# Layer 1 of four chained attention layers in narrower TensorE tiles, with its keys and values computed once per half, and another order of the first loads and of some pieces

## The chip, the cores and the metric

The kernel runs on one core of one Trainium2 chip. A core has TensorE (matrix products into PSUM), VectorE, ScalarE, GpSimd and SyncE, each with its own instruction stream, and DMA engines that move data between device memory and the on-chip memories. The metric is the device time of one execution in microseconds. The kernel before took 3054.2 us, the median of three runs (3051.49 to 3056.47).

## The reference

The input x has 4 images of 64 x 64 pixels and 64 channels, all float32. Four attention layers follow each other; the output of one is the input of the next.

```python
# layer 0: full attention, 4096 x 4096 scores per image; softmax over the last axis, then summed over the queries
q, k, v = x @ Wq + bq, x @ Wk + bk, x @ Wv + bv           # each (4096, 64)
attn = softmax(einsum('bic,bjc->bij', q, k), axis=-1)
x = gamma * einsum('bmn,bmc->bnc', attn, v) + x

# layer 1: 4096 queries of 8 channels, 1024 pooled keys and values (8 and 32 channels)
theta = x @ sn(w_theta)                                    # (4096, 8)
phi = maxpool2x2(x @ sn(w_phi))                            # (1024, 8)
g = maxpool2x2(x @ sn(w_g))                                # (1024, 32)
attn = softmax(theta @ phi.T, axis=-1)
x = x + sigma * ((attn @ g) @ sn(w_o) + b_o)

# layers 2 and 3: group norm, then full attention with 4096 x 4096 scores, projection, residual
```

`sn` divides a weight by its spectral norm estimate. The sums of exponentials are kept, and a count of partitions in which one is out of range selects a second, slower path; it does not run here.

## The kernel before, in words

An image lies on chip as 128 partitions x 2048: partitions 0 to 63 hold the 64 channels of one half of the pixels, 64 to 127 the channels of the other half. `half(i)` is a half of the partitions, `quarter(q)` 32 of them, `chunk(c)` 512 columns, `wide(j)` 1024 columns. NC is 4 (chunks), NB 32 (blocks of 128 keys).

The program is written in the order in which each engine runs it (`manual_schedule`), so the order of the Python statements is the order of each engine's queue. Foreground work is an attention of one layer for one image: `layer0`, `layer2` and `layer3` each run 64 calls of `step` (line 784). One step issues two groups of scores (`first`, lines 916 and 1115: four 64x64 products of 512 columns, then an exponential on ScalarE), and the products with the values for two earlier groups (`adds` and `then`). All other work is background: Python generators that yield MID or END, and `advance` (line 777) resumes the generator in the middle of a step, between the two groups of value products, or at its end. `background(tempo, ...)` sets which generators run under an attention; `drain` runs what is left when the attention is over. `before` and `due` are dictionaries from step number to work. Layer 1 is background: image 0's under layer 0 of image 1, with `bank=False`, because layer 0 keeps all four accumulator banks; the others' under layer 2 of the image before, with `bank=True`, an accumulator of their own.

PSUM has two buffers named s (`s_tile`, 128 x 1024 each), shared by all scores, projections and transposes, and four accumulators (`acc_tile`).

What the change touches, in the order of the file:

- `load_x` (643) loads an image in 16 DMAs (8 parts x 2 halves of the pixel blocks, for image 0). `load_form` (684) loads Wq and Wk, yields, then loads bq. For image 0 the loads of x alternate between SyncE's queue (SP) and ScalarE's; `load[0]` is ScalarE's queue until line 1394.
- `quadratic_form` (708) makes the product of Wq and Wk, and the bias column, once. `transposed` (861) turns x, `project` (826) makes queries, `first_queries` (879) the first half of image 0's queries in two arrangements, q and q_swapped.
- `layer1` (982): `project` gives theta in four copies at partitions 0, 32, 64 and 96. The loop at line 994 projects keys and values, one chunk at a time: the weight `wpg1` holds, for each of four quarters, phi in 8 columns and a quarter of g in 8 columns, so each quarter has all keys; `tensor_reduce` (1002) pools into `pg`. Eight transposes (1009) turn pg, and line 1010 copies g out of them with keys on partitions.
- `scores(j, k)` (1017): for a block of 128 keys, four products of 8 rows x 128 columns x 512, one per quarter, into two s buffers; two exponentials; from k = 1 on VectorE adds the exponentials into `zacc1` (1031). `add(j, k)` (1033) multiplies by g: into an accumulator, or, without a bank, into an s buffer, which VectorE then adds to `os[j]` (1049). `normalise` (1053) sums zacc by a product with ones (1056), takes reciprocals, and multiplies (1067); `last` (1070) applies w_o by two 128x128 products of 512 columns (1073) and adds to x1.
- The loop from line 1086 issues `scores` of unit n and `add` of unit n-1, 16 units an image and one more.
- `attention` (1106) is layer 2's and 3's loop. `turn` (1168) turns the result, copies the sums to the check columns and scales; `last` in `layer3` (1377) adds the residual and stores. At the end (1591 to 1616) the checks over all columns but the last eight run when the last attention has been issued; `rest_in_range` (1601) covers the last eight and writes the flag `bad`, called from `turn` by `after_sums`.
- At 1445 to 1456 the weights `wth1`, `wpg1` and two `wo1` are cleared and filled.

Of the kernel before, what the change touches and what calls it, by code (L numbers as in the profile page):

```python
# [11 lines left out]
ALU = mybir.AluOpType  # L12
AX = mybir.AxisListType
# [584 lines left out]
def fast_path(tc: tile.TileContext, a: dict, out: bass.AP, bad):  # L598
# [13 lines left out]
    P = 128  # L612
# [29 lines left out]

    def load_x(st, parts=((slice(None), lambda i: nc.sync.dma_start),)):
        st["xin"] = t = x_tile("xin").rearrange("p (k i c) -> p k i c", i=2, c=C)
        src = tokens(x[st["b"]])
        for ks, queue in parts:
            for r in range(4):
                for i in range(2):
                    queue(i)(t[r * W2 : (r + 1) * W2, ks, i, :], src[r, :, ks, i, :])

# [33 lines left out]
    def load_form(n, at, wq, wk, bq):  # L684
        w, b = scratch[:, at : at + P].rearrange("p (j f) -> p j f", j=2), scratch[0:C, at + P : at + P + 1]
        load[0](w[0:C, 0, :], wq)
        load[0](w[0:C, 1, :], wk)
        yield
        load[0](b, bq.rearrange("(c o) -> c o", o=1))
        form[n] = w, b, scratch[0:C, at + P + 1 : at + 3 * P + 1].rearrange("p (j f) -> p j f", j=2)  # L690

    form0 = load_form(0, 0, a["L0_conv_Wq"], a["L0_conv_Wk"], a["L0_conv_bq"])
    next(form0)
    load_x(state[0], [(ks, lambda i: (nc.sync, nc.scalar)[i].dma_start) for ks in (slice(0, 8), slice(8, 16))])
    ident = ctile([P, P], "ident")
# [28 lines left out]
    blocks = {n: (ctile([P, P], f"A{n}"), ctile([P, 1], f"Ab{n}")) for n in (0, 3)}  # L724
    for _ in form0:
        pass
    wv0 = diagonal("wv0", a["L0_conv_Wv"])
# [254 lines left out]
    def layer1(on, st, bank):  # L982
# [9 lines left out]
        rest = x_tile("pg")  # L992
        pg, g = rest[:, 0:M], rest[:, M : M + NK * 32].rearrange("p (k f) -> p k f", f=32)
        for c in range(NC):
            yield MID
            s = s_tile()
            for i in range(2):
                for d in range(2):
                    nc.tensor.matmul(  # L999
                        s[half(d), chunk(i)], wpg1[half(i), half(d)], x1[half(i), chunk(c)], start=True, stop=True  # L1000
                    )
            nc.vector.tensor_reduce(
                pg[:, ds(c * 256, 256)].rearrange("p (a b) -> p a b", b=16),
                s.rearrange("p (a i b j) -> p a b i j", i=2, b=16, j=2), AX.XY, ALU.max,
            )
        yield MID
        s = s_tile()
        for k in range(NK):
            nc.tensor.transpose(s[:, ds(k * P, P)], pg[:, ds(k * P, P)], ident)
        nc.vector.tensor_copy(  # L1010
            g.rearrange("p k (q f) -> p k q f", q=4),
            s.rearrange("p (k q f) -> p k q f", q=4, f=32)[:, :, :, D8 : 2 * D8],
        )

        ps, accs, zaccs, os = {}, {}, {}, {}

        def scores(j, k):
            ss = [s_tile() for e in range(2)]
            for e in range(2):
                for i in range(2):  # L1020
                    r = slice((2 * e + i) * 32, (2 * e + i) * 32 + D8)
                    nc.tensor.matmul(ss[e][:, chunk(i)], pg[r, ds(k * P, P)], th[r, chunk(2 * j + i)], start=True, stop=True)  # L1022
            ps[j, k] = pk = [p_tile() for e in range(2)]
            for e in range(2):
                nc.scalar.activation(pk[e], ss[e], AF.Exp)  # L1025
            if k == 1:
                zaccs[j] = x_tile("zacc1").rearrange("p (e f) -> p e f", e=2)
            if k >= 1:
                for e in range(2):
                    z = zaccs[j][:, e, :]  # L1030
                    nc.vector.tensor_tensor(z, ps[j, 0][e] if k == 1 else z, pk[e], ALU.add)  # L1031

# [37 lines left out]
        def last(j):  # L1070
            s = s_tile()
            for e in range(2):
                nc.tensor.matmul(s[:, chunk(e)], wo1[e], os[j], start=True, stop=True)  # L1073
            del os[j]
# [11 lines left out]
        for n in range(len(todo) + 1):  # L1086
            yield END if bank else MID
            if n < len(todo):
                scores(*todo[n])
            if n:  # L1090
                if not bank:
                    yield END
                add(*todo[n - 1])
            if n == NK:
                end = finish(0)
# [10 lines left out]
    def attention(st, turned_by, arranged, last, not_before, name):  # L1106
# [61 lines left out]
        def turn(c):  # L1168
# [14 lines left out]
            nc.vector.reciprocal(r_columns, z_columns)  # L1183
            if c == NC - 1 and "after_sums" in st:
                st["after_sums"]()
            t = os[c] = o_p.tile([P, 2 * 4, C], FP, tag="turned", name="turned")
# [184 lines left out]
    def layer3(st, not_before):  # L1371
# [5 lines left out]
        def last(c, t):  # L1377
            ks, i = slice(c // 2 * 8, c // 2 * 8 + 8), c % 2
            nc.vector.tensor_tensor(t, t, hb[:, ks, i, :], ALU.add)
            for r in range(4):  # L1380
                queue = nc.scalar if c == NC - 1 and st["b"] == B - 1 and r % 2 else nc.sync
                queue.dma_start(dst[r, :, ks, i, :], t[r * W2 : (r + 1) * W2, :, :])

        return attention(st, wv3, "p (i n) f -> p n i f", last, not_before, "done3")
# [6 lines left out]
    s0, s1, s2, s3 = state  # L1391
    alone(transposed("both", s0), quadratic_form(0, 1.0))
    alone(first_queries(s0))
    load[0] = nc.sync.dma_start

# [27 lines left out]

    for _ in load_form(3, 4 * P, a["L3_conv_wq"], a["L3_conv_wk"], a["L3_conv_bq"]):
        pass
    wv3, bv3 = ctile([P, P], "wv3"), ctile([P, C], "bv3")
# [19 lines left out]

    wth1, wpg1 = ctile([P, P], "wth1"), ctile([P, P], "wpg1")
    wo1 = [ctile([P, P], f"wo1_{e}") for e in range(2)]
    for t in (wth1, wpg1, *wo1):
        nc.gpsimd.memset(t, 0.0)  # L1450
    spectra = (
        ("theta", [(wth1[:, q * 32 : q * 32 + D8], every, slice(0, D8)) for q in range(4)]),
        ("phi", [(wpg1[:, q * 32 : q * 32 + D8], every, slice(0, D8)) for q in range(4)]),
        ("g", [(wpg1[:, q * 32 + D8 : q * 32 + 2 * D8], every, slice(q * D8, q * D8 + D8)) for q in range(4)]),
        ("o", [(wo1[q // 2][quarter(q), half(q % 2)], quarter(q), slice(0, C)) for q in range(4)]),
    )
# [133 lines left out]
    drain()  # L1590
    layer3(s3, free)

    last_column = checks[0]
    in_range, least = ctile([P, 2 * 4 + 2], "in_range"), ctile([P, 1], "least")
    for i, (seen, bound) in enumerate(((all_z, SUM_MAX), (all_r, 1.0 / SUM_MIN))):
        nc.vector.tensor_scalar(seen[:, 0:last_column], seen[:, 0:last_column], bound, None, ALU.is_le)
        nc.vector.tensor_reduce(in_range[:, 8 + i : 9 + i], seen[:, 0:last_column], AX.X, ALU.min)

    def rest_in_range():
        count = 2 * 4
        assert checks[0] == NCHECK and last_column == NCHECK - count
        nc.vector.tensor_scalar(in_range[:, 0:count], all_z[:, -count:], SUM_MAX, None, ALU.is_le)
# [7 lines left out]

    s3["after_sums"] = rest_in_range
    while due or urgent:
# [52 lines left out]
```

## Time and profile before

| what | value |
|---|---|
| median of three runs | 3054.2 us |
| profiled execution | 3055.06 us |
| its span, first to last instruction | 3053.3 us |
| mean granted TensorE clock | 0.997 |
| TensorE products busy | 3007.8 us, 99% |
| VectorE busy | 1775.9 us, 58% |
| ScalarE busy | 1945.8 us, 64% |
| mean DMA rate | 8 GB/s |

The page gives busy time of each engine, the span in 40 slices, the DMA queues, the chain of work that ended last, the costliest groups of instructions and the DMA issues. PE is TensorE's products, PEld its weight loads, DVE VectorE, ACT ScalarE, POOL GpSimd, SP SyncE; a q behind the name is the engine's queue. In a row of the timeline stand the start, the time taken, the engine, the line, the operation, what is written and read, shapes and a count, and in brackets the idle time before it and what ended that. A product row's bar contains a tail that overlaps the next product, so lengths of bars do not add up; starts do.

### The profile page before, as it was taken

How to read it: one execution, taken by the hardware profiler on the slowest of the kernel's cores; microseconds unless marked ns; L12 is line 12 of the kernel's file. 1: busy time of each engine (PE TensorE's matmuls, PEld its weight loads, DVE VectorE, ACT ScalarE, POOL GpSimd, SP SyncE). 2: the span in 40 equal slices, each digit the busy share in tenths (PEclk: the TensorE clock that was granted, in tenths of full speed). 3: DMA queues.
4: the chain of work that ended last, by engine and by line, in shares of the span. 5: the costliest groups of instructions: out<-in, count | busy, mean ns of one | idle time of the engine just before them, and what ended most of it. 6: DMA issues, size and time to landing. Idle time of an engine off the chain costs nothing.

```text
span 3053.3 us, 62809 instructions
## 1 busy us (share of the span) xinstructions
PE 3007.8 (99%) x27549; PEld 1133.9 (37%) x27549; DVE 1775.9 (58%) x2066; ACT 1945.8 (64%) x2815; POOL 37.0 (1%) x36
## 2 busy tenths in 40 slices
PE   8999999999999999999999999999999999999998
PEld 3333223423444442344443233333343334333333
DVE  1221332578731068772107787777887777877776
ACT  6877767665577856557885655555555555555554
POOL 0000000000000000000000000000000000000000
PEclk9999999999999999999999999999999999999999
DMA  2010000000001000000000000000000000000000
GB/s 36 1 29 1 1 1 1 15 1 1 15 1 29 1 1 1 11 5 2 15 1 1 1 1 15 19 5 5 8 19 5 19 2 1 7 17 5 8 5 9
DMA packets 41433, 24.62 MB, mean 8 GB/s; under 512 B 39744, under 2 KB 39744, under 8 KB 39744
## 3 DMA queue, kind: packets, MB, share of 16 engines
q1 hardware_dynamic: 37744, 19.77, 3.2%
q8 instruction: 218, 3.57, 0.5%
q10 hardware_dynamic: 3408, 0.76, 0.1%
q14 instruction: 63, 0.52, 0.1%
HBM read 4.79 MB, written 4.19 MB: 3 GB/s over the span
## 4 chain that ended last, share of the span: by engine, by line
PE 92%; DVE 4%; ACT 2%; issue 1%; DMA 0%; ACTq 0%; SPq 0%; DVEq 0%
PE s L1120 28%; PE acc L1154 28%; PE acc L948 14%; PE s L923 14%; PE s L1022 2%; DVE zacc L1131 2%; ACT p L1025 2%; DVE zacc L1031 1%; PE s L835 1%; PE s L1177 1%; PE s L854 1%; PE s L1073 1%; PE s L1265 0%; PE s L999 0%; ACT p L1125 0%
## 5 line engine op out<-in xcount | busy, mean ns | idle before, releaser
L1125 ACT ACTIVATE p<-s 128x1024 f32<-128x1024 f32 x1024 | 994.7, 1022 | 707.7 <-PE s L1120 699.1
L1131 DVE TENSOR_TENSOR zacc<-zacc,p 128x1024 f32<-128x1024 f32 x960 | 1173.5, 1222 | 377.3 <-ACT p L1125 339.6
L927 ACT ACTIVATE p<-s 128x1024 f32<-128x1024 f32 x512 | 519.6, 1015 | 53.1 <-PE s L923 34.1
L1154 PE MATMUL acc<-p,v 64*64 64x512 f32 x4096 | 519.0, 591 | 0.0
L948 PE MATMUL acc<-p,vs 64*64 64x512 f32 x4096 | 514.7, 591 | 1.0 <-ACT vs L937 1.0
L1120 PE MATMUL s<-q,k 64*64 64x512 f32 x2048 | 501.4, 598 | 8.9 <-ACT p L1025 5.4
L923 PE MATMUL s<-xT,q_swapped 64*64 64x512 f32 x2048 | 491.2, 592 | 6.2 <-DVE o L1049 5.7
L1154 PE MATMUL acc<-p,hT 64*64 64x512 f32 x4096 | 494.4, 590 | 0.0
L923 PE MATMUL s<-xT,q 64*64 64x512 f32 x2048 | 490.7, 592 | 2.2 <-DVE v L855 0.6
L1120 PE MATMUL s<-q,xT 64*64 64x512 f32 x2048 | 487.2, 589 | 0.0
L1120 PE MATMUL s<-q,k_swapped 64*64 64x512 f32 x2048 | 481.8, 598 | 0.7 <-DVE turned L1187 0.7
L1120 PE MATMUL s<-q,h_swapped 64*64 64x512 f32 x2048 | 479.3, 589 | 0.0
L929 DVE TENSOR_REDUCE all_z<-z 128x1 f32<-128x4 f32 x128 | 20.1, 157 | 625.1 <-ACT p L927 625.1
L937 ACT ACTIVATE vs<-v,all_r 64x64 f32<-64x64 f32 x512 | 176.6, 345 | 150.8 <-PE acc L948 73.7
L948 PEld LDWEIGHTS acc<-p,vs 64*64 64x64 f32 x4096 | 170.4, 133 | 257.1 <-issue 191.4
L1154 PEld LDWEIGHTS acc<-p,v 64*64 64x64 f32 x4096 | 172.0, 133 | 249.8 <-issue 241.3
L1154 PEld LDWEIGHTS acc<-p,hT 64*64 64x64 f32 x4096 | 157.8, 133 | 262.7 <-issue 261.9
L923 PEld LDWEIGHTS s<-xT,q_swapped 64*64 64x64 f32 x2048 | 146.7, 133 | 157.9 <-issue 111.8
L1120 PEld LDWEIGHTS s<-q,h_swapped 64*64 64x64 f32 x2048 | 144.5, 133 | 140.7 <-issue 135.0
L1120 PEld LDWEIGHTS s<-q,xT 64*64 64x64 f32 x2048 | 144.0, 133 | 139.5 <-issue 137.5
L923 PEld LDWEIGHTS s<-xT,q 64*64 64x64 f32 x2048 | 146.5, 133 | 132.3 <-issue 107.9
L1120 PEld LDWEIGHTS s<-q,k 64*64 64x64 f32 x2048 | 137.1, 133 | 157.6 <-issue 98.9
(204 smaller groups left out, 1615.3 us busy)
## 6 DMA issues: line engine op xcount, KB each, us to landing
k_swapped<-k SPq DMA_DIRECT2D x8, 512.0 KB, 5.4
h_swapped<-xT SPq DMA_DIRECT2D x8, 512.0 KB, 5.3
out_dram<-turned SPq DMA_DIRECT2D x62, 64.0 KB, 1.8
xin<-in_x_dram SPq DMA_DIRECT2D x24, 128.0 KB, 4.1
q_swapped<-q SPq DMA_DIRECT2D x6, 512.0 KB, 5.4
xin<-in_x_dram SPq DMA_DIRECT2D x8, 64.0 KB, 2.4
xin<-in_x_dram ACTq DMA_DIRECT2D x8, 64.0 KB, 2.6
out_dram<-turned ACTq DMA_DIRECT2D x2, 64.0 KB, 3.2
```

The lines of the kernel that those rows point to most:

```text
L835: nc.tensor.matmul(s[half(e), chunk(i)], w[half(i), half(e)], rhs[half(i), chunk(2 * j + (1 - e if exchanged else e))], start=True, stop=True,
L854: nc.tensor.matmul(s[:, ds(k * P, P)], rhs[:, ds((g * 8 + k) * P, P)], w, start=True, stop=True)
L923: nc.tensor.matmul(s[half(e), chunk(i)], queries(m, i, e), k[half(i), chunk(c)], start=True, stop=True)
L927: nc.scalar.activation(p, s, AF.Exp, accum_out=zs[m][:, c : c + 1])
L937: nc.scalar.activation(vs[half(e), :], v[half(e), m, :], AF.Copy, scale=rz[half(e), m : m + 1])
L948: nc.tensor.matmul(acc[c][half(i), :], vs[half(e), :], ps[2 * t + n][half(e), chunk(i)], start=(m == 0 and e == 0), stop=(m == NB - 1 and ...
L1022: nc.tensor.matmul(ss[e][:, chunk(i)], pg[r, ds(k * P, P)], th[r, chunk(2 * j + i)], start=True, stop=True)
L1025: nc.scalar.activation(pk[e], ss[e], AF.Exp)
L1120: nc.tensor.matmul(s[half(e), chunk(i)], k[(j + i) % 2][half(i), ds(j // 2 * P + e * C, C)], q[half(i), chunk(c)], start=True, stop=True,)
L1125: nc.scalar.activation(p, s, AF.Exp)
L1131: add = lambda: nc.vector.tensor_tensor(zaccs[c], p0, p, ALU.add)
L1154: nc.tensor.matmul(accs[c][e][half(i), :], v[half(e), j, :], p[half(e), chunk(i)], start=(j == 0), stop=(j == NB - 1),)
```

## The change

- The first loads: bq comes with Wq and Wk, all three on ScalarE's queue ahead of x; of x's first half only two of eight DMAs go to ScalarE's queue, the rest and the whole second half to SP's, and all later loads of weights to SP's.
- The first pieces: the quadratic form is issued ahead of the transposes; then transposes of the first half of x, its queries, the transposes of the second half, and the other arrangement of the queries.
- Layer 1's keys and values: `wpg1` is 64 columns wide, phi twice and g once in the gaps. One group of products takes two chunks, so there are two groups and two poolings per image instead of four, and `pgs[0]` holds one half of the keys in the upper 64 partitions, the other half in the lower. Two DMAs write the same with the halves exchanged into `pgs[1]`. Four transposes instead of eight, two copies instead of one, and one more yield.
- Layer 1's scores: eight products of 8 rows x 64 columns instead of four of 128 columns; the column half is the outer loop. The additions into zacc are returned as a function and called behind `add`.
- Layer 1's last products: w_o as one 128x128 tile of four 64x64 blocks, four products instead of two.
- `after_sums` becomes `after`, called when the last output's DMAs have been issued; the checks over the earlier columns run six steps before the end of the last attention.

```diff
-    form0 = load_form(0, 0, a["L0_conv_Wq"], a["L0_conv_Wk"], a["L0_conv_bq"])
-    next(form0)
-    load_x(state[0], [(ks, lambda i: (nc.sync, nc.scalar)[i].dma_start) for ks in (slice(0, 8), slice(8, 16))])
+    load_form(0, 0, a["L0_conv_Wq"], a["L0_conv_Wk"], a["L0_conv_bq"])
+    load[0] = nc.sync.dma_start
+    on_scalar = lambda r, i: nc.scalar.dma_start if i and r >= 2 else nc.sync.dma_start
+    load_x(state[0], [(slice(0, 8), on_scalar), (slice(8, 16), lambda r, i: nc.sync.dma_start)])
...
-        pg, g = rest[:, 0:M], rest[:, M : M + NK * 32].rearrange("p (k f) -> p k f", f=32)
-        for c in range(NC):
+        pgs = rest[:, 0 : M // 2], rest[:, M // 2 : M]
+        g = rest[:, M : M + NK * 32].rearrange("p (k f) -> p k f", f=32)
+        for j in range(NC // 2):
             yield MID
             s = s_tile()
             for i in range(2):
                 for d in range(2):
                     nc.tensor.matmul(
-                        s[half(d), chunk(i)], wpg1[half(i), half(d)], x1[half(i), chunk(c)], start=True, stop=True
+                        s[half(d), chunk(i)], wpg1[half(i), :], x1[half(i), chunk(2 * j + d)], start=True, stop=True
                     )
             nc.vector.tensor_reduce(
-                pg[:, ds(c * 256, 256)].rearrange("p (a b) -> p a b", b=16),
+                pgs[0][:, ds(j * 256, 256)].rearrange("p (a b) -> p a b", b=16),
                 s.rearrange("p (a i b j) -> p a b i j", i=2, b=16, j=2), AX.XY, ALU.max,
             )
+        for d in range(2):
+            nc.sync.dma_start(pgs[1][half(d), :], pgs[0][half(1 - d), :])
         yield MID
         s = s_tile()
-        for k in range(NK):
-            nc.tensor.transpose(s[:, ds(k * P, P)], pg[:, ds(k * P, P)], ident)
-        nc.vector.tensor_copy(
-            g.rearrange("p k (q f) -> p k q f", q=4),
-            s.rearrange("p (k q f) -> p k q f", q=4, f=32)[:, :, :, D8 : 2 * D8],
-        )
+        for n in range(NK // 2):
+            nc.tensor.transpose(s[:, ds(n * P, P)], pgs[0][:, ds(n * P, P)], ident)
+        by_key = s[:, 0:512].rearrange("p (k f) -> p k f", f=C)
+        nc.vector.tensor_copy(g[:, :, 0:24], by_key[:, :, 8:32])
+        nc.vector.tensor_copy(g[:, :, 24:32], by_key[:, :, 40:48])
+        yield MID
...
         def scores(j, k):
             ss = [s_tile() for e in range(2)]
-            for e in range(2):
-                for i in range(2):
-                    r = slice((2 * e + i) * 32, (2 * e + i) * 32 + D8)
-                    nc.tensor.matmul(ss[e][:, chunk(i)], pg[r, ds(k * P, P)], th[r, chunk(2 * j + i)], start=True, stop=True)
+            n, d = divmod(k, 2)
+            for m in range(2):
+                for e in range(2):
+                    for i in range(2):
+                        r = slice((2 * e + i) * 32, (2 * e + i) * 32 + D8)
+                        nc.tensor.matmul(
+                            ss[e][half(m), chunk(i)], pgs[0 if e == d else 1][r, ds(n * P + m * C, C)],
+                            th[r, chunk(2 * j + i)], start=True, stop=True,
+                        )
...
-            if k >= 1:
-                for e in range(2):
-                    z = zaccs[j][:, e, :]
-                    nc.vector.tensor_tensor(z, ps[j, 0][e] if k == 1 else z, pk[e], ALU.add)
+            zs = [ps[j, 0][e] if k == 1 else zaccs[j][:, e, :] for e in range(2)]
+            def accumulate():
+                for e in range(2):
+                    nc.vector.tensor_tensor(zaccs[j][:, e, :], zs[e], pk[e], ALU.add)
+            return accumulate
...
         def last(j):
             s = s_tile()
             for e in range(2):
-                nc.tensor.matmul(s[:, chunk(e)], wo1[e], os[j], start=True, stop=True)
+                for i in range(2):
+                    nc.tensor.matmul(s[half(i), chunk(e)], wo1[half(e), half(i)], os[j][half(e), :], start=True, stop=True)
...
-            if n < len(todo):
-                scores(*todo[n])
+            accumulate = scores(*todo[n]) if n < len(todo) else None
             if n:
                 if not bank:
                     yield END
                 add(*todo[n - 1])
+            if accumulate:
+                accumulate()
...
-    alone(transposed("both", s0), quadratic_form(0, 1.0))
-    alone(first_queries(s0))
-    load[0] = nc.sync.dma_start
+    st0 = transposed("both", s0)
+    next(st0)
+    alone(quadratic_form(0, 1.0))
+    next(st0)
+    queries0 = first_queries(s0)
+    next(queries0)
+    next(queries0)
+    alone(st0)
+    alone(queries0)
...
-    s3["after_sums"] = rest_in_range
+    s3["after"] = rest_in_range
+    before.setdefault(now[0] + NC * NB // 2 - 6, []).append(most_in_range)
+    layer3(s3, free)
```

## The prediction

> **What bounds the kernel now.** I read the page's busy times first, then its chain.
>
> ```profile
> PE 3007.8 (99%) x27549; PEld 1133.9 (37%) x27549; DVE 1775.9 (58%) x2066; ACT 1945.8 (64%) x2815; POOL 37.0 (1%) x36
> ...
> PE 92%; DVE 4%; ACT 2%; issue 1%; DMA 0%; ACTq 0%; SPq 0%; DVEq 0%
> ```
>
> TensorE is busy for 99% of the span and carries 92% of the chain, so TensorE time added or removed is span, and work of other engines counts only where TensorE waits for it. The groups of instructions by shape, TensorE only (shapes, count, busy us, mean ns), show what the change touches:
>
> ```profile
> L1022 PE MATMUL s<-th,pg 8*128 8x512 f32 x512 | 83.4, 639 | 0.2 <-ACT p L927 0.2
> L1040 PE MATMUL acc<-p,pg 128*32 128x512 f32 x384 | 51.1, 605 | 0.0
> ...
> L999 PE MATMUL s<-xT,wpg 64*64 64x512 f32 x128 | 19.1, 589 | 0.0
> ...
> L1073 PE MATMUL s<-o,wo 128*128 128x512 f32 x32 | 15.9, 618 | 0.0
> ...
> L1009 PE MATMUL s<-ident,pg 128*128 128x128 f32 x32 | 4.4, 280 | 0.0
> ```
>
> An fp32 product of 512 columns is two records. Records of one tile follow each other at 0.43 us while their own bars, with tails, are 0.59; so I measure slots, from the start of one group to the start of the next. Four 64x64 tiles run at once: 16 records (two score groups) take 1.72 us, one group of four products 0.86. Those are the pure prices below. Next, the timeline of one layer-1 unit inside an attention (images 1 to 3):
>
> ```profile
> 619.50 1.90 PE L1154 MATMUL acc<-p,v 64*64 64x512 f32 x16
> ...
> 621.33 1.14 PE L1022 MATMUL s<-th,pg 8*128 8x512 f32 x8
> ...
> 622.40 1.06 PE L1040 MATMUL acc<-p,pg 128*32 128x512 f32 x8
> 622.50 1.94 ACT L1025 ACTIVATE p<-s 128x1024 f32<-128x1024 f32 x2 [1.73 <-DVE zacc L1131]
> ...
> 623.58 0.14 PEld L1120 LDWEIGHTS s<-q,k 64*64 64x64 f32 x2 [1.02 <-ACT p L1025]
> 623.58 0.65 PE L1120 MATMUL s<-q,k 64*64 64x512 f32 x2
> ```
>
> A step runs from 617.68 to 623.58, 5.90 us, against 5.16 of pure products (1.72+1.72+0.86+0.86). The other 0.74: 0.11 ahead of L1022 (619.50 to 621.33 is 1.83, not 1.72), 0.21 between L1022 and L1040 (1.07), 0.32 behind L1040 (1.18), 0.10 within the scores. The pair behind L1040 waits for the exponential (ACT p L1025), which itself starts at 622.50, when L1022's bars end (621.33+1.14). So the end of the layer-1 scores, not only TensorE's slots, sets the step.
>
> **The change part by part.** The sum starts from the profiled execution, 3055.06 us (span 3053.3 and 1.8 around it), 0.9 above the median of 3054.2.
>
> 1. Projections of keys and values. The four groups at L999 per image become two. A slot is 0.86 (602.93 to 603.78), no wait in it: 4 images x 2 x 0.86 = 6.9. Eight pooling reductions of 1.22 on VectorE go too, off the path.
>
> 2. Eight transposes at L1009 become four. Eight take a slot of 1.02 (607.49 to 608.51), 0.16 of it the switch of tile shape: 4 x 0.43 = 1.7. Two copies replace one of 0.43 on VectorE; the added yield moves the first scores a step on, so nothing waits for them. Building the narrower weights drops one clear on GpSimd and four small products on VectorE, both idle there under layer 0: 0.
>
> 3. The swap of halves by two DMAs on SP. Nearest row: k_swapped, 512 KB, 5.4 us from issue to landing. Issued when the last reduction ends (605.4 in this stage), needed by the first scores, which the yield puts two steps later, near 613: 7.5 us of cover, and both DMAs are half that size. Cost 0. If the cover went, a TensorE wait of up to 5 us per image, 20 in all. Behind them on SP lie only the next q_swapped and k_swapped, needed a stage later.
>
> 4. Scores in 32x64 tiles: eight products where there were four, half as wide, so the same array time if all eight run together. The loads shrink from 182 ns (128 columns) to 133 (64), and the first product of a group waits for its load: L1022's first bars are 692 ns against 587 for its second, L1120's 640 against 589, so 0.105 falls to 0.05. Neighbouring tiles start 7 ns apart; four more give back 0.03 at the end. In a 5.90 step the exponential starts some 0.03 to 0.05 earlier: 48 units x 0.04 = 2. Bounds: +3 (stagger alone) and, if the array needs no switch between 64x64 and 32x64, another 64 x 0.11 = -7. No row shows two shapes with equal columns side by side, so I take the 0.11 as staying, as it does at every other switch.
>
> [...]
>
> 5. Image 0 (no PSUM bank; sums go through VectorE). Timeline of a steady step:
>
> ```profile
> 339.13 2.36 DVE L1031 TENSOR_TENSOR zacc<-zacc,p 128x1024 f32<-128x1024 f32 x2 [4.16 <-ACT p L1025]
> ...
> 340.42 0.65 PE L923 MATMUL s<-xT,q_swapped 64*64 64x512 f32 x2
> ...
> 341.41 0.68 DVE L1049 TENSOR_TENSOR o<-o,s 128x512 f32<-128x512 f32 x1
> ...
> 342.14 0.65 PE L923 MATMUL s<-xT,q_swapped 64*64 64x512 f32 x2 [0.64 <-DVE o L1049]
> ```
>
> The step is 7.12 us (333.30 to 340.42). The second score pair waits for L1049, queued behind L1031's two additions (2.36): its slot is 2.64 where unhindered ones are 1.77. With the additions behind it, L1049 runs at 340.55 to 341.23 and the 0.85 wait goes. What is late next is ScalarE: the second exponential still ends 3.3 us into the step and layer-1's second score buffer with it; with the column half outermost, the first buffer's products now also wait for that (1.1 us later than before), and L1040 for their exponential, 0.18. My step is 6.72; the trace's own steps without the VectorE wait are 6.72 too (319.92 to 326.64). Eight steps are 7.12: 8 x 0.40 = 3.2. Against it, at 411 L1067 moves behind two additions, 2.3 us, and ScalarE's L1068, and behind that the vs scalings that L948 needs, wait for it: 1.5. Net 1.7; bounds +2 and -7 (all 8 waits of 0.85).
>
> 6. Last products. Timeline, TensorE, around one:
>
> ```profile
> 713.10 1.04 PE L1154 MATMUL acc<-p,v 64*64 64x512 f32 x8
> 714.07 1.98 PE L1073 MATMUL s<-o,wo 128*128 128x512 f32 x4
> 715.98 1.09 PE L1154 MATMUL acc<-p,v 64*64 64x512 f32 x8
> ```
>
> The switch in (0.97-0.86), four 128x128 records in sequence (1.91) and the switch out (0.91-0.86) become one 64x64 group of 0.86: 0.11+1.05+0.05 = 1.2, 8 times, 9.7.
>
> 7. First loads and pieces.
>
> ```profile
> 6.82 1.94 PE L868 MATMUL s<-ident,xin 128*128 128x128 f32 x8 [6.82 <-DMA xin<-in_x_dram]
> ...
> 14.42 3.69 PE L835 MATMUL s<-xT,A 64*64 64x512 f32 x16 [0.39 <-DVE Ab L722]
> ```
>
> Transposes wait for x until 6.8; the form's steps then wait for the second evacuation, and the first queries run at 14.42, the first scores at 18.0. In the new order Wq, Wk and bq lead ScalarE's queue, so the form is done under the x loads (about 6.3, from its old 2.3 us length). Half of x, six loads on SP at about 0.5 us and two on ScalarE's queue, lands near 6.4; transposes 1.94, evacuation 0.7, queries 1.84 (the start's rate: 16 records in 3.69), which brings 11.0. The other half, eight more loads on SP, lands near 10.3, later than the 9.1 of before, yet before TensorE is free; 1.94, queries 1.84, evacuation 0.8: scores at 15.6. Gain 2.5; bounds 1 and 4. Weight loads slide some 5 us down SP's queue; constants start at 60 us, so they cost 0.
>
> 8. The end.
>
> ```profile
> 3038.75 0.55 DVE L1599 TENSOR_REDUCE in_range<-all_z 128x1 f32<-128x384 f32 x1
> ...
> 3044.55 0.15 DVE L1611 TENSOR_SCALAR bad<-s 1x1 int32<-1x1 f32 x1 [0.37 <-PE s L1610]
> ...
> 3046.18 2.11 ACTq L1382 DMA_DIRECT2D out_dram<-turned  x2
> ```
>
> The range checks over the earlier columns (1.77) leave VectorE's queue between L1139 and L1143, so L1162 starts at 40.1, not 41.2: 1.1. The rest (43.66 to 44.70) goes behind the output's issue: 1.05. ScalarE's issue of the last output, its reading of the flag and its branch end the span, so 2.1; the flag itself comes at 45.2, before ScalarE asks for it at about 46.2. Six steps earlier, VectorE absorbs 1.77 in gaps of 0.88 a step. Bounds 1 and 2.5.
>
> Sum: 6.9+1.7+2+1.7+9.7+2.5+2.1 = 26.6; 3055.1-26.6 = 3028.5, or 3027.6 beside the median. I say 3028. Least gain, each part at its bound (6.5+1.2-3-2+8+1+1) 12.7, 3041.5; most (7.5+2+9+7+10.5+4+2.5) 42.5, 3011.7.
>
> **The rivals.** *Eight tiles do not run at once, the halves follow each other.* Place: the slot of the scores, 1.07 becoming 1.9, 64 x 0.86 = 55: 3083, slower. It decides once the second half costs over 0.42 us a unit (26.6/64). For: no row shows more than four tiles at once. Against: four ran at once in all three arrangements (4x1, 2x2, 1x4). *They overlap by half*: 64 x 0.43 = 27.5, about 3056, no change. *No switch is needed* between 64x64 and 32x64: 7 less, 3021. *The swap is late*: up to 20 more, 3048 at worst.
>
> **How the numbers follow.** The forecast has 0.70, no switch 0.14, the swap late 0.03, half overlap 0.05, in sequence 0.08. Below 0.2% (6 us) a measurement of this kernel can't tell a change. Faster 0.86, same 0.05, slower 0.09. The likeliest's own range is 3014 to 3042; stretched to its outer bound and a partly late swap, 3012 to 3046. It leaves out both overlap rivals (0.13) and thin tails.
>
> **What would show it.** Right: half the records of the projections (L999's 128 to 64) and transposes (L1009's 32 to 16); scores as 1024 records with slots near 1.05 and steps of 5.8 to 5.9; last products in 0.86; image 0's steps near 6.7; first scores near 15.6; the span's end 2 us closer to the last output product. Wrong: score slots of 1.3 to 1.9, or TensorE waiting for a DMA on pg ahead of the first scores.

## The result, and the profile after

The changed kernel took 3034.9 us (median, 3034.1 to 3035.9) beside 3052.8 for the kernel before: ratio 0.9941, 95% interval 0.9924 to 0.9958. The profiled execution took 3035.91 us (span 3034.2) against 3055.06 (3053.3): 19.15 us shorter, inside the range, against a working that summed to 26.6. The question is where the missing 7.5 us went.

The page's busy line and chain:

```profile
PE 2992.7 (99%) x28013; PEld 1114.6 (37%) x28013; DVE 1765.0 (58%) x2058; ACT 1944.3 (64%) x2815; POOL 36.8 (1%) x35
...
PE 94%; ACT 3%; DVE 2%; issue 1%; DMA 0%; SPq 0%; DVEq 0%; ACTq 0%
```

TensorE is still the bound. Its groups by shape (shapes, count, busy us, mean ns of one):

```profile
L1028 PE MATMUL s<-th,pg 8*64 8x512 f32 x1024 | 85.4, 618 | 0.2 <-ACT p L925 0.2
L1054 PE MATMUL acc<-p,pg 128*32 128x512 f32 x384 | 51.1, 605 | 0.0
...
L1000 PE MATMUL s<-xT,wpg 64*64 64x512 f32 x64 | 9.9, 589 | 0.0
...
L1088 PE MATMUL s<-o,wo 64*64 64x512 f32 x64 | 8.6, 593 | 0.0
...
L1012 PE MATMUL s<-ident,pg 128*128 128x128 f32 x16 | 2.6, 286 | 0.0
```

The counts are those forecast: 1024 narrow score records, half the projections (L1000) and half the transposes (L1012). The stages give the account. A stage runs from the first scores of one layer to the first scores of the next; these are starts in the trace. The forecast column adds up the prediction's parts; the 48 units of part 4 are those of images 1 to 3, the ones with steps of 5.90. Stages without a layer 1 agree to some 0.1 us among all the executions below (the first, layer 0 of image 0, to 0.7), so small differences in the others can be read.

| stage, us of the profiled execution | before | after | shorter by | forecast |
|---|---|---|---|---|
| start, to the first scores | 18.00 | 15.55 | 2.45 | 2.5 |
| layer 0 of image 1, layer 1 of image 0 | 300.30 | 297.59 | 2.71 | 6.3 |
| layer 2 of image 0, layer 1 of image 1 | 290.14 | 286.35 | 3.79 | 5.2 |
| layer 2 of image 1, layer 1 of image 2 | 291.79 | 287.99 | 3.80 | 5.2 |
| layer 2 of image 2, layer 1 of image 3 | 289.88 | 286.00 | 3.88 | 5.2 |
| end, from the last eight score products (16 records) | 20.92 | 18.55 | 2.37 | 2.1 |
| the rest | 1842.30 | 1842.15 | 0.15 | 0 |

Start and end are as forecast; the four stages with a layer 1 fall short. First, one unit of images 1 to 3 after the change (timeline):

```profile
602.78 1.90 PE L1170 MATMUL acc<-p,v 64*64 64x512 f32 x16
...
604.61 1.11 PE L1028 MATMUL s<-th,pg 8*64 8x512 f32 x16
...
605.65 1.07 PE L1054 MATMUL acc<-p,pg 128*32 128x512 f32 x8
605.80 1.94 ACT L1034 ACTIVATE p<-s 128x1024 f32<-128x1024 f32 x2 [1.74 <-PE s L1028]
...
606.88 0.65 PE L1136 MATMUL s<-q,k 64*64 64x512 f32 x2 [0.15 <-ACT p L1034]
```

The sixteen records of the narrow scores leave a slot of 1.04 us (604.61 to 605.65), where four wide products left 1.07: all eight tiles run at once (the first eight records start within 0.05 us, 604.61 to 604.66, the second eight from 605.09). The 0.11 us at the change of tile shape stays (602.78 to 604.61 is 1.83 for 1.72). But the exponential starts 1.19 us after the scores, where it started 1.17 after them before, and the next scores at 606.88 wait for it. The slot of L1054 is 1.23, and a step is 5.91 to 5.92: no gain.

The last products, TensorE's timeline:

```profile
702.61 1.04 PE L1170 MATMUL acc<-p,v 64*64 64x512 f32 x8
703.47 1.04 PE L1088 MATMUL s<-o,wo 64*64 64x512 f32 x8
704.33 1.04 PE L1170 MATMUL acc<-p,v 64*64 64x512 f32 x8
```

They have a slot of 0.86 us (703.47 to 704.33), and so has the group ahead of them (702.61 to 703.47): no change of tile shape on either side, as forecast.

In image 0 the steady step is 6.68 us for 7.12 (6.72 was forecast). The step behind its first normalisation is 13.08 us long (400.84 to 413.92) where it was 10.13. Its timeline:

```profile
403.85 0.68 DVE L1081 TENSOR_TENSOR o<-o,r 128x512 f32<-128x512 f32 x1
404.56 0.63 ACT L1082 ACTIVATE r<-r 128x512 f32<-128x512 f32 x1 [3.86 <-DVE o L1081]
...
405.58 1.45 PE L946 MATMUL acc<-p,vs 64*64 64x512 f32 x8 [2.77 <-ACT vs L935]
...
407.21 3.00 PE L1028 MATMUL s<-th,pg 8*64 8x512 f32 x16 [0.18 <-ACT p L925]
```

VectorE's product L1081 comes behind the two moved additions, ScalarE's copy L1082, which overwrites what that product reads, waits 3.86 us for it, and L946 waits 2.77 for the scalings behind that copy. Then the scores L1028 have bars of 3.00 us in all, where other steps have 1.80. The reason is in the windows (start:end, length, busy time and instructions of PE, PEld, DVE, ACT and POOL, then the granted clock):

```profile
402.80:405.58 2.78, 0.01 (x2) 0.01 (x1) 1.73 (x2) 0.99 (x4) 0.00 (x0) 1.00 0.00 0
405.58:408.10 2.52, 2.34 (x12) 0.58 (x12) 0.00 (x0) 2.48 (x5) 0.00 (x0) 1.00 0.00 0
408.20:414.90 6.70, 6.70 (x38) 1.20 (x40) 0.84 (x2) 2.63 (x4) 0.00 (x0) 0.50 0.00 1
415.00:418.00 3.00, 3.00 (x32) 0.78 (x24) 2.15 (x3) 2.23 (x4) 0.00 (x0) 1.00 0.00 0
```

TensorE is idle for 2.78 us (0.01 busy), and from 408.17 to 415.00 its clock is at half. The prediction had 1.5 us for this place and said nothing of the clock.

### The profile page after: what moved, and what is told of

Same layout as the page of the kernel before. It is cut to its first block, busy times and chain, and to the rows that moved or that the text cites. A ratio compares the mean times of both kernels' runs of the same rounds, so it can differ in the third digit from the quotient of the medians.

```text
span 3034.2 us, 63745 instructions
## 1 busy us (share of the span) xinstructions
PE 2992.7 (99%) x28013; PEld 1114.6 (37%) x28013; DVE 1765.0 (58%) x2058; ACT 1944.3 (64%) x2815; POOL 36.8 (1%) x35
## 4 chain that ended last, share of the span: by engine, by line
PE 94%; ACT 3%; DVE 2%; issue 1%; DMA 0%; SPq 0%; DVEq 0%; ACTq 0%
PE s L1136 28%; PE acc L1170 28%; PE s L921 14%; PE acc L946 14%; PE s L1028 3%; ACT p L1034 2%; DVE zacc L1147 1%; PE s L833 1%; PE s L1054 1%; PE s L1193 1%; PE s L852 1%; PE s L1279 0%; ACT p L1141 0%; PE s L866 0%; PE s L1191 0%
## 5 line engine op out<-in xcount | busy, mean ns | idle before, releaser
L946 PE MATMUL acc<-p,vs 64*64 64x512 f32 x4096 | 516.1, 592 | 3.3 <-ACT vs L935 3.3
L1170 PE MATMUL acc<-p,v 64*64 64x512 f32 x4096 | 517.0, 593 | 0.0
L1170 PE MATMUL acc<-p,hT 64*64 64x512 f32 x4096 | 494.1, 590 | 0.0
L946 PEld LDWEIGHTS acc<-p,vs 64*64 64x64 f32 x4096 | 172.3, 133 | 259.8 <-issue 191.5
L1170 PEld LDWEIGHTS acc<-p,v 64*64 64x64 f32 x4096 | 169.6, 133 | 252.8 <-issue 247.8
L1170 PEld LDWEIGHTS acc<-p,hT 64*64 64x64 f32 x4096 | 156.6, 133 | 263.9 <-issue 263.1
```

The costliest lines, as they stand in the source:

```text
L946: nc.tensor.matmul(acc[c][half(i), :], vs[half(e), :], ps[2 * t + n][half(e), chunk(i)], start=(m == 0 and e == 0), stop=(m == NB - 1 and ...
L1170: nc.tensor.matmul(accs[c][e][half(i), :], v[half(e), j, :], p[half(e), chunk(i)], start=(j == 0), stop=(j == NB - 1),)
```

## Experiments

Theory A puts the loss on the loop order of the scores, theory B on the order of VectorE's queue, theory C on the narrow tiles themselves; D, E and F came with the results. The table gives, for each run, the median and the ratio to the kernel before (some 3055.5 us beside these runs, 3052.8 beside the changed kernel), and the stages of its profiled execution. A window is a stretch in which the granted clock is 0.50. In these stages of the kernel before and of the changed one each is 3.41 us long, and a stretch of 6.83 (408.17 to 415.00) counts as two. One costs 1.65 to 1.7 us: image 2's stage, with a window, is 1.65 longer than image 1's, without one, in the kernel before and 1.64 longer in the changed kernel, while the two are equal in e7, which has none; half of 3.41 is 1.7.

| run | median | ratio, 95% interval | image 0's stage | images 1, 2, 3 | windows in these stages |
|---|---|---|---|---|---|
| before | | | 300.30 | 290.14, 291.79, 289.88 | 1; 0, 1, 1 |
| changed | 3034.9 | 0.9941 (0.9924 to 0.9958) | 297.59 | 286.35, 287.99, 286.00 | 2; 0, 1, 1 |
| e1 buffer outermost | 3027.3 | 0.9909 (0.9894 to 0.9924) | 293.39 | 287.25, 285.59, 283.61 | 2; 1, 0, 0 |
| e2 128 columns | 3029.7 | 0.9917 (0.9903 to 0.9931) | 295.44 | 285.90, 285.92, 285.50 | 3; 0, 0, 1 |
| e3 additions first | 3040.3 | 0.9953 (0.9939 to 0.9966) | 303.77 | 286.34, 287.98, 284.33 | 1; 0, 1, 0 |
| e4 last products alone | 3045.7 | 0.9968 (0.9956 to 0.9981) | 298.22 | 289.30, 287.71, 287.43 | 1; 1, 0, 1 |
| e5 scores alone | 3063.2 | 1.0024 (1.0015 to 1.0033) | 306.88 | 292.21, 292.22, 290.24 | 0; 1, 1, 1 |
| e6 sums later | 3025.8 | 0.9900 (0.9885 to 0.9915) | 291.52 | 287.34, 285.65, 285.66 | 1; 1, 0, 1 |
| e7 both | 3017.8 | 0.9876 (0.9861 to 0.9892) | 286.42 | 284.96, 284.96, 283.29 | 0; 0, 0, 0 |
| e8 apart | 3030.0 | 0.9915 (0.9901 to 0.9928) | 286.42 | 289.17, 289.16, 287.14 | 0; 0, 0, 0 |
| e9 first between | 3014.8 | 0.9869 (0.9853 to 0.9886) | 286.43 | 284.35, 284.40, 282.36 | 0; 0, 0, 0 |
| e10 both, 128 columns | 3020.4 | 0.9887 (0.9870 to 0.9903) | 287.06 | 286.96, 285.25, 283.62 | 0; 1, 0, 0 |

**e1, the score buffer outermost.**

```diff
-            for m in range(2):
-                for e in range(2):
+            for e in range(2):
+                for m in range(2):
                     for i in range(2):
```

> The changed kernel with the loops over its scores in another order: score buffer outermost, column half inside it (the change has the column half outermost). Stages are taken from the first scores of one layer to those of the next; layer 0 of image 1 with layer 1 of image 0 beside it took 300.30 us before and 297.59 after the change, each of the three layer-2 stages with a layer 1 beside it 290.14 before and 286.35 after. Theory A (loop order): with the column half outermost neither buffer is complete until the second buffer has come free, so in image 0 the first exponential starts late; undoing the order shortens image 0's stage by 3 to 5 us (L946 behind the scores back from 1.20 to near 1.02, some 14 times, and 1 to 2 us at the step behind the normalisation) and the three others by under 0.7 each. Theory B (order of VectorE's queue) and theory C (the narrow tiles themselves): under 0.7 us in every stage.

Measured: image 0's stage is 4.20 us shorter, with two windows in both; its steady step is 6.49 instead of 6.68. The timeline of one such step, the changed kernel first, then e1, shows what moved:

```profile
335.59 1.80 PE L1028 MATMUL s<-th,pg 8*64 8x512 f32 x16
...
337.44 1.94 ACT L1034 ACTIVATE p<-s 128x1024 f32<-128x1024 f32 x2 [1.21 <-PE s L1028]
```

```profile
339.85 1.78 PE L1028 MATMUL s<-th,pg 8*64 8x512 f32 x16
...
341.01 1.94 ACT L1034 ACTIVATE p<-s 128x1024 f32<-128x1024 f32 x2 [0.51 <-PE s L1028]
```

The exponential starts 1.85 us after the scores in the changed kernel and 1.16 after them in e1. A layer-2 step is 5.88 instead of 5.91 to 5.92. The layer-2 stages move by +0.90, -2.40 and -2.39, more than was expected, but one window more or less is in each (+1, -1, -1, at 1.7 us): without these they move by -0.7 to -0.8, about the bound. Theory A holds: which buffer is complete first matters, although all eight products run at once.

**e2, 128 columns again.**

```diff
-            for m in range(2):
-                for e in range(2):
-                    for i in range(2):
...
-                            ss[e][half(m), chunk(i)], pgs[0 if e == d else 1][r, ds(n * P + m * C, C)],
+            for e in range(2):
+                for i in range(2):
...
+                        ss[e][:, chunk(i)], pgs[0 if e == d else 1][r, ds(n * P, P)],
```

> The changed kernel with its scores as four products of 128 columns again, everything else as changed: part 4 alone undone. By the prediction it is 2 us slower (48 units by 0.04). By theory A it is faster, by the same 3 to 5 us in image 0's stage as with the buffer outermost, since four products also complete one buffer after the other; in the three layer-2 stages within 0.7 us. By theory C (eight narrow tiles cost more than four wide ones by themselves) it is faster in all four stages, by over 0.7 in each; by theory B no stage moves by 0.7.

Measured: 5 us faster than the changed kernel, where the prediction's part 4 wants 2 us slower. Image 0's steady step is 6.52; its stage is only 2.15 shorter because it has three windows instead of two. Layer-2 steps are 5.90, and the layer-2 stages 0.4 to 0.5 shorter where the windows are the same. That is theory A again, and theory C falls: against e1, which differs in the tiles alone, the wide tiles are 0.02 to 0.03 us a step longer.

**e3, the additions first.**

```diff
+            if accumulate:
+                accumulate()
             if n:
                 if not bank:
                     yield END
                 add(*todo[n - 1])
-            if accumulate:
-                accumulate()
```

> The changed kernel with VectorE's additions into zacc back ahead of the addition to os: part 5 alone undone. By the prediction image 0's stage becomes 1.7 us longer. By theory B (the moved additions delay the normalisation's product, and with it ScalarE, by more than reckoned) the eight steps go from 6.68 back to 7.12 (3.5 us longer) and the step of 13.1 us back to about 10.1 (2.9 shorter): image 0's stage within 1.5 us of 297.59 on either side. By theory A most of the loss lies elsewhere, and this stage gets 2 to 4 us longer. Layer-2 stages: under 1 us each.

Measured: image 0's stage is 6.18 us longer, more than any of the three expected, and that with one window less. A steady step is 7.55, not 7.12: the late exponentials of the column half outermost and the additions ahead of L1063 add up. So the order of the additions is worth 0.87 a step beside this loop order, and theory B, that part 5 had cost more than reckoned, falls as a whole. The step behind the normalisation, though, goes back from 13.08 to 10.31, as B said.

**e4, the last products alone.**

```diff
-                nc.tensor.matmul(s[:, chunk(e)], wo1[e], os[j], start=True, stop=True)
+                for i in range(2):
+                    nc.tensor.matmul(s[half(i), chunk(e)], wo1[half(e), half(i)], os[j][half(e), :], start=True, stop=True)
```

> The kernel before with the last products alone as four 64x64 products: part 6 alone. The prediction says 9.7 us faster, 2.4 in each of the four stages with a layer 1. The rival says that the slots fall by 1.05 each but that the time comes back in part as waits of the work behind (the result's turning waited 0.81 us for a buffer in the changed kernel's layer-2 stage): 6 to 8 us.

Measured: 9.5 us in the profiled execution. By stage it is 2.08, 0.84, 4.08 and 2.45; the middle two have one window more and one less than before, and at 1.7 each all four are 2.1 to 2.5. The prediction's term holds, the rival doesn't.

**e5, the scores alone**, in the kernel before, with the column half outermost.

```diff
-            for e in range(2):
-                for i in range(2):
-                    r = slice((2 * e + i) * 32, (2 * e + i) * 32 + D8)
-                    nc.tensor.matmul(ss[e][:, chunk(i)], pg[r, ds(k * P, P)], th[r, chunk(2 * j + i)], start=True, stop=True)
+            for m in range(2):
+                for e in range(2):
+                    for i in range(2):
+                        r = slice((2 * e + i) * 32, (2 * e + i) * 32 + D8)
+                        nc.tensor.matmul(
+                            ss[e][half(m), chunk(i)], pg[r, ds(k * P + m * C, C)], th[r, chunk(2 * j + i)],
+                            start=True, stop=True,
+                        )
```

> The kernel before with its scores alone as eight 32x64 products, column half outermost (part 4 alone, in the old layout of the keys and with the old order of VectorE's additions). The prediction says 2 us faster, 0.7 of it in image 0's stage (300.30 us before). Theory A (loop order), with numbers from the three runs so far: with the old order of the additions a steady step of image 0 was 7.55 us in the run with the additions first and 7.12 before, so image 0's stage becomes 5 to 8 us longer; the layer-2 stages move by under 0.4 each, apart from windows at half clock. Theory C (narrow tiles dear in themselves): longer in all four stages.

Measured: slower than the kernel before. Image 0's stage is 6.58 longer (some 8.3 with its one window less taken into account), its steady step 7.55; the layer-2 stages are 0.4 longer once the added window of the first is taken off. Theory A has its step of 7.55, but theory C's forecast, longer in all four stages, comes true here too: this run alone doesn't tell the two apart. e1 against e2, and e7 against e10, where the tiles alone differ, do.

**e6, ScalarE's sums later.**

```diff
             nc.vector.tensor_tensor(os[j], os[j], r, ALU.mult)
+            yield MID
             nc.scalar.activation(r, r, AF.Copy, accum_out=r_column)
...
             yield from normalise(j)
             yield MID
-            yield MID
             last(j)
```

> The changed kernel with ScalarE's copy of the reciprocals, which sums them, one resumption behind VectorE's product that it has to wait for; of the two pauses ahead of the last products one goes. Theory D: in the step of 13.08 us behind the first normalisation ScalarE waits for VectorE, TensorE is then idle for 2.8 us and the clock falls to half for two windows of 3.41 us (408.17 to 415.00). Without the wait the idle time shrinks to about 1 us, both windows go or one stays, and image 0's stage becomes 3 to 6 us shorter than 297.59; in the layer-2 stages the 0.92 us that L1170 waits near the end of the layer-1 work goes. The rival (the step is long by the additions on VectorE and the exponentials alone, clock or no clock): image 0's stage within 1 us.

Measured: image 0's stage is 6.07 us shorter, just over what was expected, with one window left, at another place (311.14, among the first units). The step of 13.08 is 6.68, like its neighbours (timeline):

```profile
402.42 2.35 DVE L1043 TENSOR_TENSOR zacc<-zacc,p 128x1024 f32<-128x1024 f32 x2
...
404.43 1.80 PE L1028 MATMUL s<-th,pg 8*64 8x512 f32 x16
```

The additions still take 2.35 us, but ScalarE has its exponential at once, and L1028 has its usual 1.80. The two windows at this place went with the idle time, as theory D has it, and none stands at this place in any of the five runs with the sums later (e6 to e10); the rival falls. In the layer-2 stages another wait goes that the prediction had not named. In the changed kernel's timeline, near the end of image 1's layer 1:

```profile
727.97 0.68 DVE L1081 TENSOR_TENSOR o<-o,r 128x512 f32<-128x512 f32 x1
...
728.75 0.63 ACT L1082 ACTIVATE r<-r 128x512 f32<-128x512 f32 x1 [2.19 <-DVE o L1081]
...
729.38 1.92 ACT L1141 ACTIVATE p<-s 128x1024 f32<-128x1024 f32 x2
...
730.44 0.66 PE L1191 MATMUL s<-ident,o 128*128 128x128 f32 x4 [0.74 <-ACT p L1141]
```

ScalarE waits 2.19 us for L1081, its exponential starts late, and the turning of the result (L1191) waits 0.74 for that buffer. The step is 5.17 us long, where it is 4.36 in e6. In the kernel before a similar wait, one step later, cost 0.43 (3.86 for 3.43), so the change added some 0.4 here.

**e7, both edits**, those of e1 and e6.

```diff
-            for m in range(2):
-                for e in range(2):
+            for e in range(2):
+                for m in range(2):
...
+            yield MID
             nc.scalar.activation(r, r, AF.Copy, accum_out=r_column)
```

> Buffer outermost and ScalarE's sums later, together. If the two losses are separate, the gains add: image 0's stage near 293.4 less 3 to 6, 287.5 to 290.5; layer-2 stages near 283 without and 285 with a window at half clock. The whole about 3018 to 3022 us. If they are one loss (ScalarE late), image 0's stage stays above 292.

Measured: image 0's stage is 286.42, lower than expected, since no window is left in it either. Without the windows, at 1.7 us each, e1 gains 4.2 us there, e6 4.4 and this run 7.8, so the two losses are separate and the gains nearly add. The layer-2 stages have none, but two of them are 2 us over the 283 expected, which had been taken from the third image's stage; that one is 1.6 to 2.0 shorter than the others wherever they have the same windows.

**e8, scores and additions apart**, for all images, on top of e7.

```diff
-            yield END if bank else MID
+            yield MID
...
-                if not bank:
-                    yield END
+                yield END
                 add(*todo[n - 1])
...
-                if bank:
-                    yield MID
                 end = end if next(end, None) is not None else None
```

> As the run with both, and layer 1's scores between the two groups of value products, its addition of the unit before at the end of the step, for all images (in the change both stand at the end for images 1 to 3). Theory E: a layer-2 step with a layer-1 unit is set by ScalarE's exponential, which the next scores wait for; with a group of value products between them the wait of 0.2 us goes and a step is 5.70 instead of 5.88 to 5.92, 3 us in each layer-2 stage; and the first unit's hole of 1.1 us, which is followed by a window at half clock in 7 of 15 cases so far, nearly closes, so no such window is left in these stages: 280 to 281 us each. The rival: the switches of tile shape at one more place eat the gain, and VectorE, with four additions of 1.22 us in a step, becomes the bound: 283 or more.

Measured: 12 us slower than e7. Steps are 6.18, not 5.70. Theory E falls as to the step, and the rival's reason isn't it either: VectorE's four additions take 4.9 of the 6.18, though its number, 283 or more, is what came. The timeline shows what does:

```profile
606.11 1.94 ACT L1138 ACTIVATE p<-s 128x1024 f32<-128x1024 f32 x2 [1.51 <-PE s L1133]
...
607.69 1.50 PE L1028 MATMUL s<-th,pg 8*64 8x512 f32 x16
...
608.84 1.94 ACT L1034 ACTIVATE p<-s 128x1024 f32<-128x1024 f32 x2 [0.80 <-PE s L1028]
...
611.13 0.65 PE L1133 MATMUL s<-q,k 64*64 64x512 f32 x2
```

The scores now come one group of value products after the two attention score groups, whose second exponential ends only at 608.04 (two of 1.02 from 606.11); their slot is 1.43 instead of 1.04. With two s buffers the wait moved from the scores behind L1028 to L1028 itself, and there is one more change of tile shape: in this run's timeline the value products behind L1028 start at 609.11 and L1054 at 610.13, 1.02 for 0.86. There is no window in any of the stages.

**e9, only the first unit between**, on top of e7: the first unit has no addition behind it.

```diff
-            yield END if bank else MID
+            yield END if bank and n else MID
             accumulate = scores(*todo[n]) if n < len(todo) else None
+            if bank and n == 0:
+                yield MID
```

> The run with both, and the first unit's scores of images 1 to 3 between the two groups of value products (later units stay at the end of the step, since moving all of them lengthened each step). TensorE is idle for 1.1 us behind these scores in every run so far but the one with all units moved, because no addition of an earlier unit stands behind them. Theory F (that hole brings the windows at half clock): with the hole under 0.7 us no window is left in the layer-2 stages, and a stage is 0.4 to 0.9 us shorter than in the run with both (284.96, 284.96, 283.29). The whole 1 to 3 us shorter than 3017.8. The rival (such windows come and go without regard to the hole): one or two of them again, 1.7 us each.

Measured: 3014.8 us, the fastest, 20 us below the changed kernel and 1.3% below the one before. The layer-2 stages are 0.56 to 0.93 shorter than e7's, as expected: the first unit's step is 5.02 for 5.77. There is no window, but e7 had none either, so this run doesn't decide between theory F and its rival; what the traces say of it is in the last section.

**e10, e7 with 128 columns.**

```diff
-                for m in range(2):
-                    for i in range(2):
...
-                            ss[e][half(m), chunk(i)], pgs[0 if e == d else 1][r, ds(n * P + m * C, C)],
+                for i in range(2):
...
+                        ss[e][:, chunk(i)], pgs[0 if e == d else 1][r, ds(n * P, P)],
```

> As the run with both, but with scores as four products of 128 columns: part 4 undone where nothing else waits. The prediction has part 4 at 2 us (48 units by 0.04). From the steps of the runs with the buffer outermost and with 128 columns (5.88 and 5.90 in layer 2, 6.49 and 6.52 in image 0) it is 0.02 to 0.03 a unit, 1 to 1.5 us, if no window at half clock differs. Theory C (narrow tiles dear): this run is the faster one.

Measured: 2.7 us slower than e7 in the median. In the profiled executions the stages are longer by 0.64, 2.00, 0.29 and 0.33, the second with one window: about 1.6 us without it, 0.03 to 0.04 a step in image 0 and 0.02 in layer 2. So where their order does no harm the narrow tiles gain, and theory C falls. Of the 1.6, though, 0.9 lies in images 1 to 3, about half of what part 4 has there, and 0.64 in image 0, where it has nothing.

## Why the prediction was right in sign and short in size

- *Projections and transposes (parts 1 and 2), the swap (3).* Right: slots of 0.86 and 0.43 us less per image; the swaps land after 3.0 us and no product waits for them.
- *Scores in narrow tiles (part 4, 2 us).* Where the order does no harm the tiles gain 0.02 a unit in images 1 to 3 instead of 0.04 (e10); in this change the sign was wrong, and e2, with the wide tiles back, is 5 us faster. The step that failed is "in a 5.90 step the exponential starts some 0.03 to 0.05 earlier". It starts 0.02 later (1.19 for 1.17 us after the scores). With the column half outermost the first buffer is complete with the sixth of eight products; with the buffer outermost it is with the fourth, and in e1 the exponential starts 1.15 after the scores. The order took back more than the shorter loads (182 ns each before, 130 after) gave. In image 0, where the second buffer comes free late, it takes 0.19 a step (6.68 for 6.49). Part 5 had named that wait, but only inside the steps of 7.12.
- *Image 0 (part 5, net 1.7).* The steady step was right (6.68 for 6.72), with the loop order's cost in it, but the working counted only the eight steps of 7.12. In the trace these give 3.5 us (3.2 forecast), seven others become 0.03 to 0.53 longer, 1.45 in all (5.33, 6.43 and 6.69 in e1 against 5.63, 7.00 and 6.88 show that it is the loop order again), and the step of the normalisation 2.95 longer (1.5 forecast). 5.75 us of this step lie in a window now and 2.40 did before, which at half clock is some 1.7 of the 2.95 (half of 3.35); the wait itself, some 1.3, was near the forecast, and the clock that fell behind it had no term. Together these steps are 0.9 longer, where part 5 had 1.7 shorter.
- *Last products (part 6, 9.7).* Right: 9.5 in e4.
- *Start and end (parts 7 and 8).* Right to 0.3 us; the first scores start at 15.55 for 15.6. The hit is closer than the spread, since the eight runs on top of the change have them at 15.00 to 15.75.
- *What had no term.* The wait of L1170 near the end of layer 1 in images 1 to 3, 0.4 us each, through the same ScalarE copy; and the clock, with four windows in these stages instead of three, the added one within the 2.95.

The shortfall is thus 3.6 us in image 0's stage, 2.6 of it in the units of layer 1 and the rest in the steps behind them, not followed further, and 1.4 in each of the others, some 1.0 for the scores (0.7 forecast, 0.4 lost in e5) and 0.4 for the new wait. The end and the stages without a layer 1 give 0.4 back, which makes the 7.5. The total fell inside the range because parts 1, 2, 6, 7 and 8 were right and the losses in parts 4 and 5 stayed within their bounds (-3 and -2).

The rivals: half overlap and sequence fell at the slot of 1.04; "no switch" fell at the 1.83 that stayed; the swap was in time. The two column halves share their rows here, and the 1.04 us for sixteen records, where 1.9 was forecast for halves in sequence, shows that they do not follow each other.

## What to carry to other kernels

When a product is cut into more tiles that run at once, order them so that the buffer that is read first is complete first: the order cost more here than the tiles gave. When work is moved back in one engine's queue, look for the instruction on another engine that waits for it and stands ahead of work on the bound; ScalarE's bookkeeping copy, moved one resumption on, was worth 9 us in the medians by itself (8 between the profiled executions, the change in windows included). And measure by stages: medians alone would not have told a gain of 2 us from a window of clock.

## What the runs showed of the hardware

The clock was not expected to matter. In the traces of the kernel before and of the changed kernel the windows at half clock in these stages start at whole multiples of 3.413 us from each other: before at 418.77, 1128.75 and 1647.57, which are 208 and 152 of them apart, after at 408.17, 1114.73 and 1630.14, 207 and 151 apart. Behind the first unit's scores in layer 2, TensorE is idle for 1.1 us in ten of the kernels above (1.11 before, 1.15 in the changed kernel, 1.12 in e1), and a window follows in 15 of 30 stages; in e8 and e9, where these scores stand between the two groups of value products, in none of six.

Take the windows of a trace as grid lines, carry them on in steps of 3.413 us, and count the start of each hole from the line before it. In the kernel before, the holes of images 1, 2 and 3 start at 0.75, 2.32 and 2.11; the second and the third have a window at the next line (image 2's hole is 1127.65 to 1128.76, the window starts at 1128.75), the first has none. In the changed kernel they start at 0.49, 1.67 and 1.05, and again the second and the third have a window at the next line and the first has none. These are six holes in two executions, and no run moves a hole along the grid with all else equal: that its place there decides was not shown.

e7 has the hole too (TensorE is busy for 1.18 of the 2.30 us from 587.0 to 589.3) and no window in any of its three stages, so that none of the six stages of e8 and e9 has one is thin evidence that closing the hole keeps the clock up. Nor are length and place of a hole everything: later in image 3's stage of the kernel before, a hole of 1.22 us starts at 1803.22, 2.05 behind a line, and no window follows. No run tests what is different there.

In image 0 the order is less clear. In the kernel before, TensorE is idle for 0.64 and 0.51 us (from 412.13 and 413.85) between the lines at 411.95 and 415.36, and the window comes one period later, at 418.77. In the changed kernel 1.95 us of the 2.78 lie between the lines at 401.34 and 404.76 and the rest behind them, and the windows start one period later, at 408.17. What brings e6's window at 311.14 is open; a product's bar of 0.59 outlasts the 0.43 to the next record of its tile, so short pauses within a group of products don't show as idle time.
